# Two ends of a fused LoRA-and-adapter kernel: the first quarter's loads on two queues, and the last batch in half-width accumulators

## Chip, core and metric

The kernel runs on one core of one Trainium2 chip. The metric is device time in microseconds (us). The kernel before takes 432.92 us, the median of three runs (432.73 to 433.76).

## What is computed

Two layers with residuals over x of 8 batches, 256 tokens and 1024 features, all in float32. The first adds a dense product and a gated mixture of eight low-rank experts: the gates are a softmax over the two largest of eight logits, and the logits of one expert per batch get a bias of 5. The second adds a product with one of 16 matrices, picked per batch by an id.

```python
base = jnp.einsum('btd,od->bto', x, W)
logits = jnp.einsum('btd,ed->bte', x, Wr)
logits = logits + 5.0 * jax.nn.one_hot(language_ids, 8)[:, None, :]
topw, topi = jax.lax.top_k(logits, 2)
weights = jax.nn.softmax(topw, axis=-1)
gates = jnp.sum(jax.nn.one_hot(topi, 8) * weights[..., None], axis=-2)
h = jnp.einsum('btd,erd->bter', x, A)
lora_out = jnp.einsum('bter,bte,eor->bto', h, gates, B)                    # 8 experts of rank 16
x = x + base + 2.0 * lora_out
x = x + jnp.einsum('bsi,boi->bso', x, weight[adapter_ids])
```

## The kernel before

The features lie on the 128 partitions. A chunk k is 128 of the 1024 features, so there are eight chunks. The 2048 tokens are cut into four quarters of 512, named (j, c). The input lies in HBM so that one load brings some chunks of one quarter: `load_x(queue, i, j, c, k0, k1)` (line 104) brings chunks k0 to k1 of the half i of the features, so that i = 0 holds chunks 0 to 3 and i = 1 chunks 4 to 7. One chunk of a quarter is 128 rows of 2 KB, 256 KB. `load_aw` (line 112) brings pieces of a table of 136 columns per chunk, which holds the experts' A and the router's Wr side by side; a chunk of it is 68 KB.

The stages, in the order in which TensorE runs them:

- Ten warm-up matmuls on an identity matrix (line 539).
- `project(j, c)`, four times: for each chunk k and each of four groups of 128 tokens one matmul of 128 by 136 columns (line 198). It gives the router's logits and the experts' h of one quarter. After the first quarter's matmuls stands `use_ids()`: VectorE casts the ids to float (line 154), a small matmul spreads them over the partitions (line 156), and VectorE makes the bias from them (lines 158 and 164). The logits get the bias in one addition (line 174), and ScalarE copies h out (line 217).
- The dense product and the LoRA part as seven products of a Strassen-like scheme over 2 by 2 blocks, each of which is itself a scheme of seven steps with accumulators A, B and X (line 374). VectorE makes the sums and differences of blocks (line 174), and results leave PSUM through `evict` (line 360, ScalarE) or an addition (VectorE).
- `adapt(u)` for the eight batches, again seven steps each, of 128 by 512 columns (line 479). `mm` writes an accumulator, `evict` or `add` takes it into the tile z, and `store` (line 491) sends z out. `load_w1` loads the next batches' matrices.

Each engine works through its own queue in the order in which the program was written, and waits on semaphores. Loads are issued from two queues that share the same 16 DMA engines: SP's (`nc.sync`) and ACT's (`nc.scalar`). Eight semaphores are dealt out in turn to the DMAs of these two, so that the ninth load waits until the first has landed: the issue of chunks 4 and 5 of the first quarter waits for the first piece of the table.

The order of the first loads, as written in lines 114 to 126: ACT issues the table in pieces of chunks 0, 1 to 2, and 3 to 7, and after them the two rows of ids (lines 123 and 124). SP issues x chunk 0, chunk 1, chunks 2 to 3, chunks 4 to 5, chunks 6 to 7, and then the second quarter and the rest. Each chunk's matmuls wait for their piece of the table and their piece of x.

The last batch differs in its end: its c22 half is stored early, and the last accumulator, 128 by 512 in one bank of PSUM, is taken out in two halves, one by ScalarE (line 529) and one by VectorE (line 530), each with a store of its own on ACT's and SP's queue.

Of the kernel before, what the change touches and what calls it, by code (L numbers as in the profile page):

```python
# [25 lines left out]
def kernel(  # L26
# [25 lines left out]
    nc = tc.nc  # L52
# [5 lines left out]
    NB = lang.shape[1]  # L58
    NAD = w1.shape[0]
    S = 256  # L60
    KC = D // P
    KH = KC // 2
    TH = NB * S // 2
    TQ = TH // 2
    OG = O // 2
# [3 lines left out]
    SH = S // 2  # L69
# [16 lines left out]
    def bank(name):  # L86
        return psum.tile([P, 2, TQ], F32, name=name, tag="acc")
# [5 lines left out]
    def xk(k, j, c):  # L93

        return xb[f"{k // KH + 1}{j+1}"][:, k % KH, c * TQ : (c + 1) * TQ]
# [5 lines left out]
    ids = const.tile([1, 2, NB], I32, name="ids")  # L101

    def load_x(queue, i, j, c, k0, k1):
        queue.dma_start(  # L104
            xb[f"{i+1}{j+1}"][:, k0:k1, c * TQ : (c + 1) * TQ], xT[i, j, c, :, k0:k1, :]
        )
# [4 lines left out]
    def load_aw(queue, k0, k1):  # L111
        queue.dma_start(aw_sb[:, k0:k1, :], awT[:, k0:k1, :])

    load_aw(nc.scalar, 0, 1)
    load_x(nc.sync, 0, 0, 0, 0, 1)
    load_aw(nc.scalar, 1, 3)
    load_x(nc.sync, 0, 0, 0, 1, 2)
    load_aw(nc.scalar, 3, 8)
    load_x(nc.sync, 0, 0, 0, 2, 4)
    load_x(nc.sync, 1, 0, 0, 0, 2)  # L120
    load_x(nc.sync, 1, 0, 0, 2, 4)
    load_x(nc.sync, 0, 0, 1, 0, 4)
    nc.scalar.dma_start(ids[:, 0, :], lang)
    nc.scalar.dma_start(ids[:, 1, :], adapt)
    load_x(nc.sync, 1, 0, 1, 0, 4)
    load_x(nc.sync, 0, 1, 0, 0, 4)
    load_x(nc.sync, 1, 1, 0, 0, 4)
# [16 lines left out]
    nc.vector.tensor_copy(desc, desc_i)  # L144
    ecol = const.tile([P, E], F32, name="ecol")
    nc.vector.tensor_copy(ecol, ecol_i)
    ids_f = const.tile([1, 2 * NB], F32, name="ids_f")
    bias = const.tile([P, NB, E], F32, name="bias")
    aid_i = const.tile([1, NB], I32, name="aid_i")
# [3 lines left out]
    def use_ids():  # L153
        nc.vector.tensor_copy(ids_f, ids.rearrange("o t b -> o (t b)"))
        wide = bank("ids_wide")[:, 0, :NB]
        nc.tensor.matmul(wide, lhsT=ones, rhs=ids_f[:, :NB], start=True, stop=True)  # L156

        nc.vector.tensor_tensor(
            bias,
            wide.unsqueeze(2).to_broadcast([P, NB, E]),  # L160
            ecol.unsqueeze(1).to_broadcast([P, NB, E]),
            ALU.is_equal,
        )
        nc.vector.tensor_scalar(bias, bias, LANG_BIAS, None, ALU.mult)
# [11 lines left out]
    def add(out_, x, y):  # L176
        tt(out_, x, y, ALU.add)
# [14 lines left out]
    def project(j, c):  # L192

        ps = bank(f"ps_h_{j}_{c}")
        for k in range(KC):
            for r in range(CQ):
                v, u = divmod(r, 2)
                nc.tensor.matmul(  # L198
                    ps[:, v, u * EA : (u + 1) * EA],
                    lhsT=xk(k, j, c)[:, ts(r, P)],  # L200
                    rhs=aw_sb[:, k, :],
                    start=(k == 0 and u == 0),
                    stop=(k == KC - 1),
                    skip_group_check=True,
                )
        if (j, c) == (0, 0):
            use_ids()
        ps = ps[:, :, : 2 * EA].rearrange("p v (u e) -> p v u e", u=2)
        split = lambda t: t[:, c * CQ : (c + 1) * CQ, :].rearrange("p (v u) e -> p v u e", v=2)
        nb = CQ * P // S  # L210
        b0 = (2 * j + c) * nb
        add(
            split(lg[j]),
            ps[:, :, :, ER:],
            bias[:, b0 : b0 + nb, :].unsqueeze(2).to_broadcast([P, nb, CQ // nb, E]),
        )
        nc.scalar.copy(split(hT[j]), ps[:, :, :, :ER])
# [72 lines left out]
    def pump(place, last=7):  # L290

        share = sum(t[0] for t in todo) / (last - place + 1)
        i = 0
        while i < len(todo) and (share > 0.3 or place == last):
            if todo[i][1] > place:
                i += 1
                continue
            us, _, fn = todo.pop(i)
            fn()
            share -= us  # L300
# [4 lines left out]
    def pieces(fn, out_, x, y, n):  # L305

        w = KH // n
        cut = lambda t, c: t[:, c * w : (c + 1) * w, :]
        return [
            (1.22, 0, lambda c=c: fn(cut(out_, c), cut(x, c), cut(y, c))) for c in range(n)  # L310
        ]
# [45 lines left out]
    def evict(dest, acc, base=None):  # L357

        if base is None:
            nc.scalar.copy(dest, acc)  # L360
        else:
            add(dest, acc, base)
# [57 lines left out]
    sums, adapter = {}, {}  # L420
    order = [b for b in range(NB // 2, NB)] + [b for b in range(NB // 2)]

    def load_w1(u, *which):
        if u >= NB:
            return
        if u not in adapter:
            b = order[u]
            adapter[u] = nc.sync.value_load(aid_i[0:1, b : b + 1], min_val=0, max_val=NAD - 1)
        for ij in which:
            i, g = int(ij[0]) - 1, int(ij[1]) - 1  # L430
            nc.sync.dma_start(
                rawset[u % 2][ij], w1[bass.ds(adapter[u], 1), g, i].rearrange("a p k n -> p (a k) n")
            )
# [11 lines left out]
    def yhalf(b):  # L445

        j, r = divmod(b, NB // 2)
        c, s = divmod(r, 2)

        def half(i, k):  # L450
            v = yq(f"{k+1}{j+1}").rearrange("p (r c) m n -> p r c m n", c=2)[:, :, c]
            return v[:, :, :, s * S + i * SH : s * S + (i + 1) * SH]

        return half
# [13 lines left out]
    def adapt(u):  # L468
        b = order[u]
        half = yhalf(b)  # L470
        s1, s2, s3, s4 = sums[u]
        w = rawset[u % 2]
        accs = {}

        def mm(name, lhs, rhs, first=False):
            if first:
                accs[name] = bank(f"{name}1_{u}")[:, 0, :]
            for k in range(KH):
                nc.tensor.matmul(  # L479
                    accs[name],  # L480
                    lhsT=lhs[:, k // 2, k % 2, :],
                    rhs=rhs[:, k, :],
                    start=(first and k == 0),
                    stop=(k == KH - 1),
                    skip_group_check=True,
                )
            return accs[name]

        def store(i, o0=0, o1=O, queue=nc.sync):
            r = b * S + i * SH  # L490
            queue.dma_start(out[r : r + SH, o0:o1], z[i][:, o0:o1])

        z = [
            pool.tile([P, O], F32, name=f"z_{u}_{i}", tag=tag)
            for i, (pool, tag) in enumerate(((sub1, "t1"), (sub1, "t3")) if u % 2 else ((sub2, "t2"), (sub2, "t2")))
        ]
        c11, c12, c21, c22 = (z[i][:, ts(j, OG)] for i in range(2) for j in range(2))
        evict(c11, mm("A", half(0, 0), w["11"], True))
        for t in pieces(minus, w["11"], w["t"], w["11"], 2):
            t[2]()  # L500
        pump(1)
        evict(c22, mm("B", s1, w["12"], True))
        load_w1(u + 2, "12")
        pump(2)
        evict(c12, mm("A", s2, w["t"]))
        for t in pieces(minus, w["t"], w["21"], w["t"], 2):
            t[2]()
        pump(3)
        add(c11, mm("X", half(0, 1), w["21"], True), c11)
        load_w1(u + 2, "21")  # L510
        pump(4)
        add(c22, mm("A", s3, w["11"]), c22)
        if u + 1 == NB:
            store(1, OG, O)
        load_w1(u + 2, "11")
        pump(5)
        add(c12, mm("B", s4, w["22"]), c12)
        store(0)
        load_w1(u + 2, "22")
        pump(6)  # L520
        if u + 1 < NB:
            evict(c21, mm("A", half(1, 1), w["t"]))
            store(1)
            pump(7)
            return

        acc = mm("A", half(1, 1), w["t"])
        m = OG // 2
        nc.scalar.copy(c21[:, :m], acc[:, :m])  # L529
        nc.vector.tensor_copy(c21[:, m:], acc[:, m:])  # L530
        store(1, 0, m, nc.scalar)
        store(1, m, OG)


    ctx.enter_context(tc.manual_schedule())
# [2 lines left out]
    for i in range(WARM):  # L538
        nc.tensor.matmul(idle[:, 0, :P], lhsT=ident, rhs=ident, start=True, stop=True)
    project(0, 0)  # L540
    project(0, 1)
    use_adapter_ids()
    for t in gating(0):
        t[2]()
    project(1, 0)
    add_identity(wb["11"])
    for t in make_subs("1", "11", "11"):
# [46 lines left out]
    for u in range(NB):  # L594
        if u + 1 < NB:
            todo += prep_y(u + 1)
            todo += prep_w1(u + 1, 4)
        adapt(u)
# [48 lines left out]
```

## Time and profile before

| | |
|---|---|
| median of three runs | 432.92 us |
| the profiled execution | 433.07 us |
| its span from first to last instruction | 431.3 us |
| TensorE busy in the span | 424.4 us (98%) |
| VectorE busy | 270.5 us (63%) |
| ScalarE busy | 32.5 us (8%) |
| bytes moved | 55.81 MB, 129 GB/s in the mean |
| queue of SP | 12048 packets, 54.92 MB |
| queue of ACT | 580 packets, 0.69 MB |

The page gives for each group of instructions the line, the engine, the operation, its tiles, the count, the busy time, the mean duration of one and the idle time of the engine before it with what ended that. PE is TensorE's matmuls, PEld its weight loads, DVE is VectorE, ACT is ScalarE, POOL is GpSimd, SP is SyncE; a q behind the name is the sequencer that issues DMAs. One matmul in float32 makes two records. Times in the timeline count from the start of the span.

What the engines did in the stages of the span (for each engine the busy us and the number of records):

```profile
core 0: us, PE busy (x) PEld busy (x) DVE busy (x) ACT busy (x) POOL busy (x), PEclk, DMA share, GB/s
0.00:15.40 15.40, 12.16 (x86) 11.61 (x86) 0.47 (x4) 0.00 (x0) 0.88 (x8) 1.00 0.86 292
15.40:38.00 22.60, 22.60 (x196) 22.59 (x196) 12.18 (x36) 3.25 (x5) 0.00 (x0) 1.00 1.03 400
38.00:235.00 197.00, 197.00 (x472) 88.10 (x471) 141.76 (x156) 10.72 (x12) 0.00 (x0) 1.00 0.12 44
235.00:403.40 168.40, 168.40 (x393) 74.48 (x392) 108.70 (x122) 15.83 (x27) 0.00 (x0) 1.00 0.53 190
403.40:431.30 27.90, 24.24 (x57) 10.45 (x55) 7.40 (x8) 2.72 (x5) 0.00 (x0) 1.00 0.15 57
```

The rows are the first quarter's projection with what lies ahead of it, the other three quarters, the seven products of the first layer, seven batches of the second layer, and the last batch with its stores. In the three middle rows TensorE is busy for the whole of the stage. In the second row the DMA engines are, too: their share is 1.03 at 400 GB/s.

### The profile page before, as it was taken

What the parts mean: (1) busy time and instruction counts of PE and PEld (TensorE: products, weight loads), DVE (VectorE), ACT (ScalarE), POOL (GpSimd) and SP (SyncE); (2) the same over time, 40 slices, a digit from 0 to 9 for tenths busy, and PEclk for the clock granted to TensorE, in tenths of its full rate; (3) what the DMA queues carried; (4) which work ended last, traced back from release to release, by engine and by line L of the source; (5) the groups of instructions that cost most, each with busy time, mean ns of one, the idle gap of its engine ahead of it and who ended that gap; (6) DMA issues with size and microseconds to landing.
All of it is one profiled execution on the core that took longest, in us unless ns stands there. A gap on an engine that the chain in (4) does not pass through costs nothing.

```text
span 431.3 us, 3166 instructions
## 1 busy us (share of the span) xinstructions
PE 424.4 (98%) x1198; PEld 207.2 (48%) x1198; DVE 270.5 (63%) x325; ACT 32.5 (8%) x49; POOL 0.9 (0%) x8
## 2 busy tenths in 40 slices
PE   6999999999999999999999999999999999999996
PEld 6997444444444444444444444444444444444442
DVE  0068695743538887999765775575756576665521
ACT  0112210002000000000000101010110101010110
POOL 0000000000000000000000000000000000000000
PEclk9999999999999999999999999999999999999999
DMA  7995000000002040150202266555738476550202
GB/s 250 390 406 226 0 2 0 0 0 0 2 0 97 14 180 2 52 206 35 97 2 97 97 238 217 216 207 201 286 125 304 157 259 226 198 195 0 97 0 98
DMA packets 12643, 55.81 MB, mean 129 GB/s; under 512 B 1108, under 2 KB 1620, under 8 KB 8020
## 3 DMA queue, kind: packets, MB, share of 16 engines
q1 hardware_dynamic: 12048, 54.92, 35.3%
q10 hardware_dynamic: 580, 0.69, 0.5%
q8 instruction: 9, 0.15, 0.1%
q14 instruction: 6, 0.05, 0.0%
HBM read 47.22 MB, written 8.39 MB: 129 GB/s over the span
## 4 chain that ended last, share of the span: by engine, by line
PE 97%; DMA 2%; SPq 0%; DVE 0%; ACT 0%; issue 0%
PE A L479 25%; PE A L374 24%; PE B L374 14%; PE B L479 13%; PE X L374 7%; PE ps_h L198 7%; PE X L479 6%; DMA x<-xT_dram 2%; PE ps_g L271 0%; SPq L104 0%; DVE z L530 0%; ACT z L529 0%; PE ids_wide L156 0%
## 5 line engine op out<-in xcount | busy, mean ns | idle before, releaser
L479 PE MATMUL B<-x,x 128*128 128x512 f32 x128 | 57.5, 592 | 0.0
L374 PE MATMUL A<-t,s 128*128 128x512 f32 x112 | 50.3, 592 | 0.0
L479 PE MATMUL A<-w,x 128*128 128x512 f32 x96 | 43.2, 592 | 0.0
L479 PE MATMUL A<-w,y 128*128 128x512 f32 x96 | 42.7, 592 | 0.0
L479 PEld LDWEIGHTS B<-x,x 128*128 128x128 f32 x128 | 24.3, 190 | 30.6 <-issue 30.6
L174 DVE TENSOR_TENSOR w<-w,w 128x1024 f32<-128x1024 f32 x24 | 29.1, 1223 | 15.4 <-PE A L479 15.3
L174 DVE TENSOR_TENSOR y<-A,y 128x1024 f32<-128x1024 f32 x22 | 26.9, 1223 | 17.1 <-PE A L374 17.1
L374 PEld LDWEIGHTS A<-t,s 128*128 128x128 f32 x112 | 21.3, 190 | 26.8 <-issue 26.8
L198 PE MATMUL ps_h<-y,x 128*128 128x136 f32 x256 | 30.7, 280 | 1.8 <-DMA y<-awT_dram 1.0
L360 ACT COPY z<-A 128x512 f32<-128x512 f32 x23 | 13.5, 586 | 246.8 <-PE A L479 246.8
L198 PEld LDWEIGHTS ps_h<-y,x 128*128 128x128 f32 x256 | 29.9, 190 | 2.3 <-DMA y<-awT_dram 1.2
L479 PEld LDWEIGHTS A<-w,x 128*128 128x128 f32 x96 | 18.2, 190 | 23.0 <-issue 23.0
L479 PEld LDWEIGHTS A<-w,y 128*128 128x128 f32 x96 | 18.2, 190 | 23.0 <-issue 23.0
L374 PE MATMUL A<-x,w 128*128 128x512 f32 x56 | 25.2, 592 | 0.0
L374 PE MATMUL X<-x,w 128*128 128x512 f32 x56 | 25.2, 592 | 0.0
L374 PE MATMUL B<-x,s 128*128 128x512 f32 x56 | 25.2, 592 | 0.0
L374 PE MATMUL A<-t,w 128*128 128x512 f32 x56 | 25.2, 592 | 0.0
L374 PE MATMUL B<-t,s 128*128 128x512 f32 x56 | 25.2, 592 | 0.0
L174 DVE TENSOR_TENSOR y<-B,y 128x1024 f32<-128x1024 f32 x12 | 14.7, 1224 | 16.3 <-PE B L374 16.3
L174 DVE TENSOR_TENSOR y<-X,y 128x1024 f32<-128x1024 f32 x7 | 8.6, 1226 | 18.0 <-PE X L374 18.0
L174 DVE TENSOR_TENSOR x<-x,x 128x1024 f32<-128x1024 f32 x16 | 18.9, 1218 | 0.0
L174 DVE TENSOR_TENSOR t<-x 128x1024 f32<-128x1024 f32 x14 | 17.1, 1220 | 0.0
(96 smaller groups left out, 378.2 us busy)
## 6 DMA issues: line engine op xcount, KB each, us to landing
x<-w_dram SPq DMA_DIRECT2D x24, 1024.0 KB, 4.8
w<-w_dram SPq DMA_DIRECT2D x8, 1024.0 KB, 4.7
out_dram<-z SPq DMA_DIRECT2D x15, 512.0 KB, 3.3
x<-xT_dram SPq DMA_DIRECT2D x6, 1024.0 KB, 11.2
w<-wT_dram SPq DMA_DIRECT2D x4, 1024.0 KB, 15.6
x<-xT_dram SPq DMA_DIRECT2D x3, 512.0 KB, 6.4
x<-xT_dram SPq DMA_DIRECT2D x2, 256.0 KB, 5.0
b_sb<-bT_dram SPq DMA_DIRECT2D x1, 512.0 KB, 14.8
```

What stands on the lines that cost most here:

```text
L174: nc.vector.tensor_tensor(out_, x, y, op)
L198: nc.tensor.matmul(ps[:, v, u * EA : (u + 1) * EA], lhsT=xk(k, j, c)[:, ts(r, P)], rhs=aw_sb[:, k, :], start=(k == 0 and u == 0), stop=(k ...
L360: nc.scalar.copy(dest, acc)
L374: nc.tensor.matmul(acc[:, m, :], lhsT=l, rhs=r, start=(first and i < 2), stop=(i >= len(steps) - 2), skip_group_check=True,)
L479: nc.tensor.matmul(accs[name], lhsT=lhs[:, k // 2, k % 2, :], rhs=rhs[:, k, :], start=(first and k == 0), stop=(k == KH - 1), skip_group_c ...
```

## The change

Three edits. The first quarter's x loads go out by turns on SP and ACT, chunks 0 to 3 in pieces of one chunk, and the table's last piece moves from ACT to SP. The two rows of ids are issued from GpSimd's queue, behind its own set-up work, and `use_ids()` moves from behind the first quarter's matmuls to before chunk 4. The last batch has a function of its own, `adapt_last`: each step runs as two halves of 256 columns, whose accumulators lie in the two banks of one tile, each half taken out as soon as it is done; the last half leaves through ScalarE alone, and all of its stores are on SP's queue.

```diff
     load_aw(nc.scalar, 0, 1)
     load_x(nc.sync, 0, 0, 0, 0, 1)
     load_aw(nc.scalar, 1, 3)
-    load_x(nc.sync, 0, 0, 0, 1, 2)
-    load_aw(nc.scalar, 3, 8)
-    load_x(nc.sync, 0, 0, 0, 2, 4)
+    load_x(nc.scalar, 0, 0, 0, 1, 2)
+    load_x(nc.sync, 0, 0, 0, 2, 3)
+    load_aw(nc.sync, 3, 8)
+    load_x(nc.scalar, 0, 0, 0, 3, 4)
     load_x(nc.sync, 1, 0, 0, 0, 2)
-    load_x(nc.sync, 1, 0, 0, 2, 4)
+    load_x(nc.scalar, 1, 0, 0, 2, 4)
     load_x(nc.sync, 0, 0, 1, 0, 4)
-    nc.scalar.dma_start(ids[:, 0, :], lang)
-    nc.scalar.dma_start(ids[:, 1, :], adapt)
...
     ecol = const.tile([P, E], F32, name="ecol")
     nc.vector.tensor_copy(ecol, ecol_i)
+    nc.gpsimd.dma_start(ids[:, 0, :], lang)
+    nc.gpsimd.dma_start(ids[:, 1, :], adapt)
...
         for k in range(KC):
+            if (j, c, k) == (0, 0, KH):
+                use_ids()
             for r in range(CQ):
...
-        if (j, c) == (0, 0):
-            use_ids()
...
+        if u + 1 == NB:
+            adapt_last(b, half, sums[u], w, z)
+            return
...
-        if u + 1 == NB:
-            store(1, OG, O)
...
-        if u + 1 < NB:
-            evict(c21, mm("A", half(1, 1), w["t"]))
-            store(1)
-            pump(7)
-            return
-
-        acc = mm("A", half(1, 1), w["t"])
+        evict(c21, mm("A", half(1, 1), w["t"]))
+        store(1)
+        pump(7)
+
+    def adapt_last(b, half, sy, w, z):
+        s1, s2, s3, s4 = sy
         m = OG // 2
-        nc.scalar.copy(c21[:, :m], acc[:, :m])
-        nc.vector.tensor_copy(c21[:, m:], acc[:, m:])
-        store(1, 0, m, nc.scalar)
-        store(1, m, OG)
+        accs = {}
+
+        def mm(name, lhs, rhs, first=False):
+            if first:
+                accs[name] = bank(f"{name}1_last")
+            for v in range(2):
+                for k in range(KH):
+                    nc.tensor.matmul(
+                        accs[name][:, v, :m],
+                        lhsT=lhs[:, k // 2, k % 2, :],
+                        rhs=rhs[:, k, v * m : (v + 1) * m],
+                        start=(first and k == 0),
+                        stop=(k == KH - 1),
+                        skip_group_check=True,
+                    )
+                yield v
...
+        def step(i, j, plus, name, lhs, rhs, first=False):
+            for v in mm(name, lhs, rhs, first):
+                c = place(i, j, v)
+                evict(c, accs[name][:, v, :m], c if plus else None)
+
+        step(0, 0, False, "A", half(0, 0), w["11"], True)
+        for t in pieces(minus, w["11"], w["t"], w["11"], 2):
+            t[2]()
+        step(1, 1, False, "B", s1, w["12"], True)
+        step(0, 1, False, "A", s2, w["t"])
+        for t in pieces(minus, w["t"], w["21"], w["t"], 2):
+            t[2]()
+        step(0, 0, True, "X", half(0, 1), w["21"], True)
+        store(0, 0, OG)
+        step(1, 1, True, "A", s3, w["11"])
+        store(1, OG, O)
+        step(0, 1, True, "B", s4, w["22"])
+        store(0, OG, O)
+        for v in mm("A", half(1, 1), w["t"]):
+            evict(place(1, 0, v), accs["A"][:, v, :m])
+            store(1, v * m, (v + 1) * m)
```

More of the change, by code (lines that the diff above doesn't have):

```diff
@@ L487, in mm, with store @@
             return accs[name]
-        def store(i, o0=0, o1=O, queue=nc.sync):
+        def store(i):
             r = b * S + i * SH
-            queue.dma_start(out[r : r + SH, o0:o1], z[i][:, o0:o1])
+            nc.sync.dma_start(out[r : r + SH, :], z[i])
         z = [
@@ L520, in adapt, with place, store @@
         pump(6)
-        if u + 1 < NB:
-            evict(c21, mm("A", half(1, 1), w["t"]))
-            store(1)
-            pump(7)
-            return
-        acc = mm("A", half(1, 1), w["t"])
-        m = OG // 2
-        nc.scalar.copy(c21[:, :m], acc[:, :m])
-        nc.vector.tensor_copy(c21[:, m:], acc[:, m:])
-        store(1, 0, m, nc.scalar)
-        store(1, m, OG)
+        evict(c21, mm("A", half(1, 1), w["t"]))
[3 more added lines that the diff above has]
+        s1, s2, s3, s4 = sy
+        m = OG // 2
+        accs = {}
[13 more added lines that the diff above has]
+                yield v
+        def place(i, j, v):
+            o = j * OG + v * m
+            return z[i][:, o : o + m]
+        def store(i, o0, o1):
+            r = b * S + i * SH
+            nc.sync.dma_start(out[r : r + SH, o0:o1], z[i][:, o0:o1])
+        def step(i, j, plus, name, lhs, rhs, first=False):
[18 more added lines that the diff above has]
+            store(1, v * m, (v + 1) * m)
     ctx.enter_context(tc.manual_schedule())
```

## The prediction

> **What bounds the kernel now.** I read the page's busy shares first, then the chain that ended last, then the costliest groups with the waits, then the timeline of the two ends.
>
> ```profile
> PE 424.4 (98%) x1198; PEld 207.2 (48%) x1198; DVE 270.5 (63%) x325; ACT 32.5 (8%) x49; POOL 0.9 (0%) x8
> ...
> PE 97%; DMA 2%; SPq 0%; DVE 0%; ACT 0%; issue 0%
> ...
> L198 PE MATMUL ps_h<-y,x 128*128 128x136 f32 x256 | 30.7, 280 | 1.8 <-DMA y<-awT_dram 1.0
> ```
>
> TensorE holds 97% of the chain, and its only idle time above a rounding is 1.8 us before the projection (L198). So a change can gain in two places: those 1.8 us, and what lies after the last matmul. In between TensorE has no gap, so whatever the start gains or loses arrives undiminished at the end. The start, from the timeline of PE (start, duration, group, idle before it):
>
> ```profile
> 5.17 1.13 PE L198 MATMUL ps_h<-y,x 128*128 128x136 f32 x8
> 7.29 1.19 PE L198 MATMUL ps_h<-y,x 128*128 128x136 f32 x8 [0.98 <-DMA y<-awT_dram]
> 9.34 5.83 PE L198 MATMUL ps_h<-y,x 128*128 128x136 f32 x48 [0.86 <-DMA x<-xT_dram]
> 15.10 0.38 PE L156 MATMUL ids_wide<-ids_f,ones 1*128 1x8 f32 x2
> 15.41 0.85 PE L198 MATMUL ps_h<-y,x 128*128 128x136 f32 x5
> ```
>
> A chunk k is four matmuls, eight records. Chunk 0 starts at 5.17 behind the warm-up, chunk 1 waits to 7.29, chunk 2 to 9.34, and chunks 2 to 7 run without a stop: (15.10 - 9.34) / 6 = 0.96 us each. The second block starts at 15.41. When the loads land, from the issues in two short stretches (KB, us from issue to landing; by the timeline of the queues the four of the first stretch were issued at 1.66, 1.67, 1.20 and 1.18, the last one at 5.09):
>
> ```profile
> q1 hardware_dynamic: 317, 0.59, 57.2%
> q10 hardware_dynamic: 275, 0.22, 22.1%
> ...
> x<-xT_dram SPq DMA_DIRECT2D x1, 512.0 KB, 7.6
> y<-awT_dram ACTq DMA_DIRECT2D x1, 340.0 KB, 7.4
> x<-xT_dram SPq DMA_DIRECT2D x1, 256.0 KB, 5.9
> y<-awT_dram ACTq DMA_DIRECT2D x1, 136.0 KB, 6.1
> ...
> x<-xT_dram SPq DMA_DIRECT2D x1, 512.0 KB, 5.6
> ```
>
> So x chunk 1 lands at 7.10, aw 1-2 at 7.28, aw 3-7 at 9.07, x chunks 2-3 at 9.26, x chunks 4-5 at 10.69; the stretch after shows 512 KB in 6.4 from 5.51, chunks 6-7 at 11.91. The first two lines, of 1.5 to 5.5 us, matter most: SP's queue moved 317 packets, 0.59 MB, ACT's 275, 0.22 MB. The queues take turns by packet, not by byte, with ACT slightly behind. The other end:
>
> ```profile
> 427.67 0.37 ACT L529 COPY z<-A 128x256 f32<-128x256 f32 x1 [13.15 <-PE A L479]
> 428.08 0.38 ACTq L491 DMA_DIRECT2D out_dram<-z  x1
> 428.08 0.42 DVE L530 COPY z<-A 128x256 f32<-128x256 f32 x1 [3.08 <-ACT z L529]
> 428.53 0.33 SPq L491 DMA_DIRECT2D out_dram<-z  x1
> ```
>
> PE ends at 427.65. VectorE's half copy waits for ScalarE's half, since both read one accumulator bank. The last store is issued at 428.53, lands 1.9 us later (both final stores show 1.9), and the span ends at 431.3.
>
> **What the Trainium skill says.** "DMA: Bandwidth & Descriptors", section "Queues, rings and completion order": each DMA engine goes round its queue rows packet by packet; the packet counts above agree. Same page, "Issuing engines are not separate DMA queues": issuing from several engines saves only issue time. SP and ACT both carry loads from 0.74 us on already, so a second queue is nothing new here; only what stands at which place in each is. "PSUM — Partial Sum Buffer", "PSUM bank collisions raise a hardware error": two engines may not touch one bank at once, which is why L530 waits for L529. "TensorE: Matmul & The Clock Gate", "Part 1": the clock is halved after an idle window of about 3.4 us; no gap here is that long and the page's clock row is 9 throughout.
>
> **The change part by part.**
>
> Order of first loads. Each piece of one chunk is 128 rows over 16 DMA engines, 8 packets each. Before, rounds of 8 were: x0 with aw0; x1 with aw1-2; half of x2-3 with aw3-7; the rest. So chunk 1 was ready after round 2. After, SP carries x0, x2, aw3-7, then x4-5 (which waits for aw0's semaphore, at 5.09 as now); ACT carries aw0, aw1-2, x1, x3, x6-7. Round 2 is x2 with aw1-2: the same packet sizes as before, so it ends near 7.3, but with chunk 2 landed and not chunk 1. Chunk 1 comes in round 3, beside aw3-7: the bytes of today's round 3, on the lagging queue. So I put it where aw3-7 landed, at 9.07. PE starts chunk 1 at 9.11, where it now starts chunk 2 at 9.34; it is one chunk short, and 0.23 us ahead: 0.96 - 0.23 = +0.73. The bounds: if the 8 packets that x2-3 has alone after aw3-7 cost not the 0.19 between the landings but their full share (256 KB at the 370 GB/s of 7.2 to 9.3, an estimate, 0.71), it is +0.25; if a slow DMA engine delays round 3 by half a us, +1.2.
>
> Is anything later still late? Chunk 2 (landed) runs at 10.07. Chunk 3 at 11.03 needs x3: round 4, 1824 KB in all, between 1568 KB at 9.26 and 2080 KB at 10.69, so about 9.97. Chunk 4 needs x4-5 after round 5; x6-7's first half goes beside it, so 2336 KB: halfway to 2592 KB at 11.91, 11.30, against a start at 11.99. Chunk 6 needs 2848 KB, about 12.5, against 14.22. The second block's 1 MB is as far back in bytes as now (7.26 + 7.6 = 14.86) and is needed at 16.14. All hidden. SP's later loads wait for semaphores of pieces that land up to 1 us later, while the queue is backed up (DMA share 1.0 from 12 to 28 us): nothing.
>
> Ids over GpSimd's queue. Leaves two tiny issues (0.56 and 0.24 us) off ACT, where nobody waits. POOL is free from 1.44 us and nothing stands behind it. ids_wide moves ahead of chunk 4, so PE would wait for ids there: needed at 11.99, landed now before the cast at 7.91. No row of before shows a load on this queue; the DMA page, "Anatomy of one DMA", gives about 2 us fixed. Taken as 0; the cover is 10 us, beyond it each us costs one. Below nothing it cannot go: the 0.31 of the ids matmul is paid in either place while PE is the late side. DVE's bias and lg work moves ahead of the block's end, off the path.
>
> Last batch in halves. 28 matmuls of 512 columns become 56 of 256; records 56 to 112. Today 3.43 us for 8 records of 1024 column passes at 2.4 GHz is 0.429 = 0.4267 + 0.0024. At 512 passes with the same remainder 0.2158: 112 x 0.2158 - 56 x 0.429 = +0.14. No row shows 256 columns. The nearest, 136 columns, makes a record in 0.96 / 8 = 0.120 with its weight load, so weight loads hide below 0.216. Bounds: 0, and +0.7 with a remainder of 0.007 as at 136 columns. The doubled small copies and adds stand beside matmuls; VectorE's and ScalarE's idle before their last rows is 3.1 and 13.1.
>
> The end. The last half's copy is 0.37 alone on ScalarE, then SP issues: 0.02 + 0.37 + 0.04 after PE's end, where it is 0.88 now (428.53 - 427.65). -0.45, with the store's landing unchanged at 1.9. The first half's store goes 1.7 us earlier and clears. What is late next is this copy and the store's own landing.
>
> Sum: +0.73 + 0.14 - 0.45 = +0.42 on the profiled execution's 433.07 (span 431.3 and 1.8 around it): 433.49. It stands 0.15 above the median of 432.92, so I forecast 433.3.
>
> **Rivals.** (1) Chunk 1 does come early: ACT is served by bytes or ahead of SP, and x1 lands near 7.3. For it: ACT's pieces are smaller. Against it: the packet counts. Even then chunks 1 to 3 end by 10.3 and chunk 4 waits for x4-5 at 11.30, which x6-7 now shares the engines with: 11.34 + 4 x 0.96 = 15.18 against 15.41 (ids hidden), so -0.23; in all 433.07 - 0.23 + 0.14 - 0.45 = 432.5, or 432.4 on the median. Only loads about 1 us quicker altogether make it 431.4. (2) Slower, by the clock: PE is idle from 6.30 to 9.11, 2.8 us. If chunk 1 lands after 9.7, the gap is 3.4 us and the clock is halved for the next 3.4 us. The gap costs 0.6 more, the clock 1.7: 433.3 + 2.3 = 435.6. Against it: a gap of 2.8 cannot hold a whole window. (3) The new queue is late: ids land after 11.99. At 13.5 us it is 1.5: 434.8. (4) The edit of the loads does nothing, x1 being as early as now with nothing else moved: only the end, 432.6.
>
> **Numbers.** Forecast 62% (its own range 432.6 to 434.1: start +0.25 to +1.2, end -0.45 to +0.25); (1) 19%, half of it with somewhat quicker loads and so a third of it under 431.6; (2) 8%; (3) 4%; (4) 7%. 0.3%, about what a measurement of this kernel can tell from no change, is 1.3 us: faster lies below 431.6, slower above 434.2. Faster: a third of (1) and a little of (4), 8%. Slower: (2), (3) and the forecast's tail, 13%. Same: 79%. Range 431.9 to 434.2.
>
> **What would show it.** Right: chunk 1's matmuls start near 9.1 with one gap of about 2.8 us put down to x; chunks 1 to 3 run on; ids_wide costs 0.3 before chunk 4; the second block starts near 16.1; each step of the last batch takes 3.45; PE's end to the last issue is 0.43. Wrong: chunk 1 near 7.3, a gap before chunk 4, projection rows at twice their time after the gap, or PE waiting for ids_f. A forecast below 432 fails with the packet turns; one above 434.2 with the clock.

## The result: slower by 5 us, and where the profile after puts it

The changed kernel takes 438.07 us, the median of five runs (437.87 to 438.35), against 433.01 for the kernel before beside it: a ratio of 1.0115, interval 1.01 to 1.013. (Ratios and intervals come from comparing all runs of two kernels, so they differ a little from the ratio of the two medians.) The forecast was 433.3 in a range of 431.9 to 434.2, that is no change that could be told from none; the kernel is 5 us slower. The spans of the two profiled executions are 431.3 and 436.3 us: the whole difference is inside the span.

The page's busy times and chain for the kernel after:

```profile
PE 426.2 (98%) x1254; PEld 217.3 (50%) x1254; DVE 270.6 (62%) x327; ACT 33.4 (8%) x53; POOL 2.0 (0%) x10
...
PE 97%; DMA 1%; ACT 0%; DVE 0%; issue 0%; ACTq 0%; DVEq 0%
```

TensorE is busy 1.8 us more, in 56 more records, and the span is 5.0 us longer. So some 3 us are new idle time of TensorE. The shares in percent do not show it: they still say 98% and 97%. The start is not where the time was lost (timeline of PE, kernel after):

```profile
5.25 1.15 PE L202 MATMUL ps_h<-y,x 128*128 128x136 f32 x8
8.28 3.02 PE L202 MATMUL ps_h<-y,x 128*128 128x136 f32 x24 [1.88 <-DMA x<-xT_dram]
11.23 0.38 PE L158 MATMUL ids_wide<-ids_f,ones 1*128 1x8 f32 x2
11.54 5.71 PE L202 MATMUL ps_h<-y,x 128*128 128x136 f32 x47
```

The two gaps of before, 0.98 and 0.86, have become one of 1.88, and the rest runs without a stop. Before the last batch the kernel after is 0.16 us ahead: its first matmul there starts at 403.44, where that of before starts at 403.60, in the middle of a row of two steps (chain in order of time, before and then after):

```profile
400.17 6.87 PE A L479 x16
...
424.20 3.45 PE A L479 x8
```

```profile
403.44 1.74 PE A_last L540 x8
...
431.04 2.01 PE A_last L540 x8
```

The loss is in the last batch (timeline, kernel after, the last two steps: TensorE's matmuls and the copies and additions between them):

```profile
424.45 1.89 PE L540 MATMUL B_last<-x,x 128*128 128x256 f32 x8
...
426.38 0.42 DVE L176 TENSOR_TENSOR z<-B_last,z 128x256 f32<-128x256 f32 x1 [1.30 <-PE B_last L540]
...
426.86 1.99 PE L540 MATMUL B_last<-x,x 128*128 128x256 f32 x8 [0.52 <-DVE z L176]
...
428.69 1.89 PE L540 MATMUL A_last<-w,y 128*128 128x256 f32 x8
...
430.62 0.37 ACT L362 COPY z<-A_last 128x256 f32<-128x256 f32 x1 [14.18 <-PE A_last L540]
431.04 1.99 PE L540 MATMUL A_last<-w,y 128*128 128x256 f32 x8 [0.46 <-ACT z L362]
433.07 0.37 ACT L362 COPY z<-A_last 128x256 f32<-128x256 f32 x1 [2.08 <-PE A_last L540]
```

Read a step from its first matmul to the next step's. Eight records of the first half, then a gap that ends with the copy (or the addition) of the first half, then the second half. The edit was meant to let the second half's matmuls run beside the first half's copy; the second half waits for it, in every one of the seven steps. TensorE's last record ends at 433.05 in the kernel after and at 427.65 in that of before. So the seven steps take 433.05 - 403.44 = 29.61 us where those of before took 427.65 - 403.60 = 24.05: +5.56. From there to the end of the span it is 436.3 - 433.05 = 3.25 instead of 3.65: -0.40. With the start's -0.16 that is +5.0, the difference of the spans.

### The profile page after: what moved, and what is told of

It reads as the page before. It is cut to its first block, busy times and chain, and to the rows that moved or that the text cites. A ratio compares the mean times of both kernels' runs of the same rounds, so it can differ in the third digit from the quotient of the medians.

```text
span 436.3 us, 3288 instructions
## 1 busy us (share of the span) xinstructions
PE 426.2 (98%) x1254; PEld 217.3 (50%) x1254; DVE 270.6 (62%) x327; ACT 33.4 (8%) x53; POOL 2.0 (0%) x10
## 4 chain that ended last, share of the span: by engine, by line
PE 97%; DMA 1%; ACT 0%; DVE 0%; issue 0%; ACTq 0%; DVEq 0%
PE A L376 24%; PE A L481 22%; PE B L376 14%; PE B L481 11%; PE X L376 7%; PE ps_h L202 7%; PE X L481 6%; PE A_last L540 3%; PE B_last L540 2%; DMA x<-xT_dram 1%; PE X_last L540 1%; ACT z L362 0%; PE ps_g L273 0%; DVE z L176 0%; ACTq L112 0%
## 5 line engine op out<-in xcount | busy, mean ns | idle before, releaser
L481 PE MATMUL B<-x,x 128*128 128x512 f32 x112 | 50.3, 592 | 0.0
L481 PE MATMUL A<-w,x 128*128 128x512 f32 x88 | 39.6, 592 | 0.0
L481 PE MATMUL A<-w,y 128*128 128x512 f32 x88 | 39.1, 592 | 0.0
L481 PEld LDWEIGHTS B<-x,x 128*128 128x128 f32 x112 | 21.3, 190 | 26.8 <-issue 26.8
L362 ACT COPY z<-A 128x512 f32<-128x512 f32 x21 | 12.3, 587 | 241.1 <-PE A L481 241.1
L481 PEld LDWEIGHTS A<-w,y 128*128 128x128 f32 x88 | 16.7, 190 | 21.0 <-issue 21.0
L481 PEld LDWEIGHTS A<-w,x 128*128 128x128 f32 x88 | 16.7, 190 | 21.0 <-issue 21.0
L376 PEld LDWEIGHTS B<-x,s 128*128 128x128 f32 x56 | 10.6, 190 | 13.4 <-issue 13.4
```

The source lines that it names most:

```text
L376: nc.tensor.matmul(acc[:, m, :], lhsT=l, rhs=r, start=(first and i < 2), stop=(i >= len(steps) - 2), skip_group_check=True,)
L481: nc.tensor.matmul(accs[name], lhsT=lhs[:, k // 2, k % 2, :], rhs=rhs[:, k, :], start=(first and k == 0), stop=(k == KH - 1), skip_group_c ...
```

## The experiments

The theory after the result: the loss is one wait per step, for the copy of the first half, and the program sets it because both halves lie in one tile, although in two banks of PSUM; the new loads change next to nothing. The main rival: narrow matmuls, with twice as many weight loads, are slow in themselves. A second one: the start has a gain or a loss of about 1 us, hidden by the other part.

**The loads alone.** The kernel before with the first two edits.

```diff
-    load_x(nc.sync, 0, 0, 0, 1, 2)
-    load_aw(nc.scalar, 3, 8)
-    load_x(nc.sync, 0, 0, 0, 2, 4)
+    load_x(nc.scalar, 0, 0, 0, 1, 2)
+    load_x(nc.sync, 0, 0, 0, 2, 3)
+    load_aw(nc.sync, 3, 8)
+    load_x(nc.scalar, 0, 0, 0, 3, 4)
...
+    nc.gpsimd.dma_start(ids[:, 0, :], lang)
+    nc.gpsimd.dma_start(ids[:, 1, :], adapt)
...
```

> The kernel before with the new order of loads and the ids on GpSimd's queue, last batch as before. Theory (all of the loss is in the last batch; at the start chunk 1 comes a DMA round later and the later chunks follow without a stop, which about cancels): within 0.5 us of before, 432.6 to 433.5. Rival (the loads cost the +0.73 that was forecast and the last batch the rest): 433.6 to 433.9. Rival (the loads gain 1 us or more, hidden behind a larger loss): 431.5 to 432.0.

Measured: 433.13 us against 432.89, a ratio of 1.0002, interval 0.9993 to 1.0011. Neither +0.73 nor a gain of 1 us is inside it (-0.3 to +0.5).

**The last batch alone.** The kernel before with the third edit.

```diff
+        if u + 1 == NB:
+            adapt_last(b, half, sums[u], w, z)
+            return
...
```

> The kernel before with the last batch in halves alone, loads and ids as before. Theory (a wait of TensorE for the first half's eviction in each of seven steps, about 0.8 us each, 0.45 given back at the end): before plus 5.1, 438.0 to 438.4. Rival (start and last batch share the loss): clearly under 437.5.

Measured: 438.07 us against 432.89, 1.0117, interval 1.0103 to 1.0132. All of the loss is here.

**Halves in tiles of their own.** The kernel after; first halves of A and B in the two banks of one tile, second halves in those of another, X's in two more. Same matmuls, same copies, same order.

```diff
             if first:
-                accs[name] = bank(f"{name}1_last")
+                if name != "B":
+                    tiles[name] = [bank(f"{name}1_last_{v}") for v in range(2)]
+                accs[name] = [tiles[{"B": "A"}.get(name, name)][v][:, int(name == "B"), :m] for v in range(2)]
...
```

> The kernel after, with each half's accumulator in a tile of its own (first halves of A and B in the two banks of one tile, second halves in those of another, X's in two more). Theory (the wait is one that is set per tile, though the halves lie in two banks): no gap between the halves, a step at 3.45 to 3.50 us, 432.3 to 433.0. Rival (256-column matmuls with twice the weight loads are slow in themselves, or the waits follow the banks): steps stay near 4.2 us and the time near 438.

Measured: 432.56 us against 432.89, 0.9991, interval 0.9985 to 0.9998. The seven steps of this kernel's last batch in the chain in order of time (start, us, what) and the end of the timeline:

```profile
403.56 10.36 PE A_last L542 x48
413.92 3.45 PE X_last L542 x16
417.38 10.37 PE A_last L542 x48
```

```profile
424.12 3.62 PE L542 MATMUL A_last<-w,y 128*128 128x256 f32 x16
...
426.05 0.37 ACT L362 COPY z<-A_last 128x256 f32<-128x256 f32 x1 [11.71 <-PE A_last L542]
427.77 0.37 ACT L362 COPY z<-A_last 128x256 f32<-128x256 f32 x1 [1.35 <-PE A_last L542]
```

(The first rows carry A's name for B's steps too, which share its tiles.) All 112 records run as one chain, 48 of them in 10.36 us, 3.45 a step. The first half's copy at 426.05 now lies beside the second half's matmuls, and TensorE does not stop for it. The matmuls and weight loads are those of the kernel after, 1254 records of each in both, so the rival falls: it was the tile. Rid of the wait, the change as a whole is worth some 0.3 us.

**Both halves, then out.** The kernel after, one tile, but each step's two halves are computed before either is taken out.

```diff
-            for v in mm(name, lhs, rhs, first):
+            for v in list(mm(name, lhs, rhs, first)):
                 c = place(i, j, v)
...
-        for v in mm("A", half(1, 1), w["t"]):
+        for v in list(mm("A", half(1, 1), w["t"])):
```

> The kernel after, with both halves of a step computed before either is taken out; same matmuls and same one tile. Theory (the wait comes from taking the first half out between the two): steps at 3.45 to 3.50 us, the end as late as before, 432.9 to 433.5. Rival (narrow matmuls and weight loads cost it): near 438.

Measured: 433.12 us against 432.89, 1.0002, interval 0.9994 to 1.0011. In its chain every step but the last is 3.45, and the seven together take 24.19 us, as they do with tiles of their own (427.75 - 403.56): the narrow matmuls cost 24.19 - 24.05 = 0.14.

**One wait.** As that run, but in the last step the first half is taken out between the two.

```diff
-        for v in list(mm("A", half(1, 1), w["t"])):
+        for v in mm("A", half(1, 1), w["t"]):
```

> The kernel after, where steps 1 to 6 of the last batch are taken out after both halves, and only in the last step the first half is taken out between the two. Theory (each eviction between the halves costs TensorE some 0.75 us, seven of them made the loss; in the last step it gives back 0.4 at the end): 0.3 above the run that takes out all after both halves, 433.2 to 433.7. Rival (the loss needs the chain of seven): same as that run or 0.4 below it, 432.7 to 433.1.

Measured: 433.36 us against 433.09, 1.0008, interval 1.0 to 1.0016. The median is 0.24 above that of the run before it, but the kernel before measured beside it is 0.20 higher too, and the two intervals overlap, so the times do not tell the two runs apart. The chain in order of time does:

```profile
420.69 3.45 PE B_last L540 x16
424.14 1.74 PE A_last L540 x8
425.88 0.02 issue
425.91 0.38 ACT z L362
426.29 0.04 issue
426.33 2.01 PE A_last L540 x8
```

The one step with a wait takes 428.34 - 424.14 = 4.20 instead of 3.47: 0.73. Of this 0.44 is the copy and its two handovers, and 0.27 is in the second half itself, 2.01 instead of 1.74. Seven such waits are 5.1; the seven of the kernel after cost 5.42 (29.61 - 24.19). The three that wait for VectorE's additions cost 0.78 to 0.85 each, the four that wait for copies 0.73 to 0.78. So even in the one step where splitting is of use, with one tile it costs 0.73 and saves 0.4 at the end (431.6 - 428.34 = 3.26 from TensorE's last record to the end of the span, against 431.5 - 427.83 = 3.67).

**Chunk 1 and chunk 2 change places** in the loads, with tiles of their own. Now the question is whether the start has more to give.

```diff
-    load_x(nc.scalar, 0, 0, 0, 1, 2)
-    load_x(nc.sync, 0, 0, 0, 2, 3)
+    load_x(nc.sync, 0, 0, 0, 1, 2)
+    load_x(nc.scalar, 0, 0, 0, 2, 3)
```

> The kernel with halves in tiles of their own, and in its loads x chunk 1 and chunk 2 change places (chunk 1 on SP behind chunk 0, chunk 2 on ACT behind the table's second piece). Theory (queues take turns by packet, so the second place of either queue lands a round before the third; then chunks 4 and 5, which share the engines with 6 and 7, set the pace at about 11.3 us): chunk 1 starts at 6.4 to 7.1, a new gap stands before chunk 4, which starts near 11.4, and the time is at most 0.3 us below that with tiles of their own, 432.2 to 432.6. Rival (the first pieces are all that matters at the start): chunk 4 follows without a gap near 10.4 and the time is 431.4 to 431.7.

Measured: 432.46 us against 433.09, 0.9986, interval 0.9977 to 0.9994. Timeline of PE:

```profile
5.39 2.40 PE L202 MATMUL ps_h<-y,x 128*128 128x136 f32 x16
8.33 2.12 PE L202 MATMUL ps_h<-y,x 128*128 128x136 f32 x16 [0.54 <-DMA x<-xT_dram]
10.38 0.38 PE L158 MATMUL ids_wide<-ids_f,ones 1*128 1x8 f32 x2
11.43 6.75 PE L202 MATMUL ps_h<-y,x 128*128 128x136 f32 x56 [0.67 <-DMA x<-xT_dram]
```

As the theory said: chunk 1 follows chunk 0 at once, and a new gap of 0.67 stands before chunk 4, which starts at 11.43 where the kernel after had it at 11.54. Another of 0.54 stands before chunk 2.

**Chunks 6 and 7 behind 4 and 5 on SP,** on top of that, with tiles of their own, and once more in the kernel before without any change of its last batch.

```diff
-    load_x(nc.scalar, 1, 0, 0, 2, 4)
+    load_x(nc.sync, 1, 0, 0, 2, 4)
```

> As the run before, and chunks 6 and 7 go back to SP behind chunks 4 and 5. Theory (by the bytes ahead of it, chunk 4's piece lands near 10 us): no gap before chunk 4, the second block starts at 14.3 to 14.9 instead of 15.5, 431.4 to 432.0. Rival (start-up of the DMA engines, not the order, sets when a piece lands): as with the loads of the change, 432.4 to 432.7.

> The kernel before, its last batch untouched, with ids on GpSimd's queue and the loads of the run before last (chunks 1, 4, 5, 6, 7 on SP, chunks 2 and 3 on ACT). Theory: the gain of the order alone, 0.6 to 1.1 us under before, 431.8 to 432.4. Rival (order of no effect): 432.8 to 433.2.

Measured: 432.67 us against 433.09, 0.9991, interval 0.9983 to 0.9999; and for the loads alone 433.04 against 433.09, 0.9999, interval 0.999 to 1.0007. The theory missed: no gain. The gap had moved again, to chunks 2 and 3, and chunk 4 starts at 11.50 and 11.77 (timeline of PE of the first of the two):

```profile
8.66 1.19 PE L202 MATMUL ps_h<-y,x 128*128 128x136 f32 x8 [0.66 <-DMA x<-xT_dram]
10.09 1.17 PE L202 MATMUL ps_h<-y,x 128*128 128x136 f32 x8 [0.24 <-DMA x<-xT_dram]
11.19 0.38 PE L158 MATMUL ids_wide<-ids_f,ones 1*128 1x8 f32 x2
11.50 6.75 PE L202 MATMUL ps_h<-y,x 128*128 128x136 f32 x56
```

The load of chunks 4 and 5 no longer waits for a semaphore in this order (SP issues it at 2.14 us, and not at 5.27 as in the run before), so it shares the engines with chunk 3, which lands at 10.0.

**Chunks 4 and 5 on ACT, 6 and 7 on SP,** with chunks 1 and 2 changed over and tiles of their own as above, and then the same with only accumulator A in halves.

```diff
-    load_x(nc.sync, 1, 0, 0, 0, 2)
-    load_x(nc.scalar, 1, 0, 0, 2, 4)
+    load_x(nc.scalar, 1, 0, 0, 0, 2)
+    load_x(nc.sync, 1, 0, 0, 2, 4)
```

> Halves in tiles of their own and chunk 1 and 2 changed over, and now chunks 4 and 5 take ACT's place behind chunk 3 while 6 and 7 go to SP. Theory (a piece lands by the packets ahead of it in both queues; before, 6 and 7 landed at 10.2 from that place and 4 and 5 at 11.4): no gap before chunk 4, second block at 14.4 to 14.8, 431.5 to 432.0, about 0.7 below the run with the two chunks changed over. Rival (all orders end at the same 15.3, since what counts is the sum of bytes before the last chunks): 432.3 to 432.6.

> As the run before, but only accumulator A is in halves (two tiles), B and X in whole width of 512. Theory (a step in halves costs 0.02 more than a whole one): 0.1 below the run before, not to be told from it, 431.4 to 432.0. Rival (the halves of B and X also gave something): above it by more than 0.3.

Measured: 432.26 us against 433.00, 0.9980, interval 0.9972 to 0.9988; and 432.29, 0.9983, interval 0.9975 to 0.9991. These two have the lowest times of all, 0.2% under the kernel before. The timeline of PE of the first:

```profile
5.84 4.91 PE L202 MATMUL ps_h<-y,x 128*128 128x136 f32 x32
10.68 0.38 PE L158 MATMUL ids_wide<-ids_f,ones 1*128 1x8 f32 x2
11.34 6.87 PE L202 MATMUL ps_h<-y,x 128*128 128x136 f32 x57 [0.28 <-DMA x<-xT_dram]
```

Its theory missed in part: chunks 0 to 3 run on, but a gap of 0.28 is left before chunk 4, and the time lies above the 432.0 that it allowed, next to the rival's 432.3. The second time is 0.03 above the first, so halves of B and X are worth nothing that can be measured. Whether these loads or only the tiles make them better than the run with tiles of their own (0.9985 to 0.9998) stays open, as the intervals touch.

**The kernel before once more,** profiled only.

> The kernel before, profiled again. Theory (the 9.07 us at which the table's last piece landed in the first profile was one slow DMA engine; in the run with the last batch alone changed it was 8.5): the chunks from 2 on start at 8.6 to 9.0. Rival (9.3 is what this order gives): 9.2 to 9.4.

Measured: 433.27 us, and the timeline of PE has

```profile
5.84 2.81 PE L198 MATMUL ps_h<-y,x 128*128 128x136 f32 x16
9.51 5.83 PE L198 MATMUL ps_h<-y,x 128*128 128x136 f32 x48 [0.86 <-DMA x<-xT_dram]
```

My theory of one chance slow DMA engine fails: chunk 2 starts at 9.51, later than in the first profile (9.34); in the run with the last batch alone changed, the same loads had it at 8.85. The scatter is real, but 9.3 is no outlier for this order.

## Why the prediction was wrong, step by step

Term by term, forecast against measured: the start +0.73 against -0.16, the last batch +0.14 against +5.56, the end -0.45 against -0.40.

**The last batch in halves: the failed step.** It said that the doubled small copies and adds "stand beside matmuls" and priced the edit at +0.14. The price of the matmuls was exact: 24.19 against 24.05, +0.14. The forecast took a record of 256 columns as half of one of 512 but for a small remainder, 0.2158, and 24.19 / 112 is 0.216. What failed is the overlap, whose price was put at nothing: the cover was named without asking whether the program lets the two run beside each other. The second half's first matmul waits for the copy or addition of the first half, 0.73 to 0.85 us in each of seven steps. It was taken for granted that different banks mean no wait; the Trainium skill ("PSUM — Partial Sum Buffer", "PSUM bank collisions raise a hardware error") says that accesses to different banks run clean, and with tiles of their own the copy at 426.05 does lie beside the matmuls, so the chip has no objection. The wait is the program's, and it goes by the tile: the same matmuls and copies with other tiles take 432.56 us. It cost 5.42 us, on the path that sets the end, where TensorE has no slack at all. The kernel before had a sign of such a wait, VectorE's half copy behind ScalarE's. The prediction put it down to the bank; both halves lay in one bank of one tile there, so that row could not tell the two apart, and no run tried to.

**The end: right.** The forecast was 0.43 from PE's end to the last issue and -0.45. Measured in the kernel after: PE's end at 433.05, the copy at 433.07 for 0.37, the last issue at 433.47, and the span's end 0.40 closer to PE's end than before.

**The start: right in outline, wrong in one term.** One gap instead of two, put down to x; chunks 1 to 3 without a stop; the ids matmul 0.31 before chunk 4; chunk 4's piece near 11.30 (issued at 5.18, landed 6.2 later): all as forecast. The term that was mis-sized is chunk 1's landing, taken from where the table's last piece landed before, 9.07. In the kernel after it is 1.68 + 6.5, 8.1 to 8.2 (issues of the kernel after):

```profile
x<-xT_dram ACTq DMA_DIRECT2D x2, 256.0 KB, 6.5
...
y<-awT_dram ACTq DMA_DIRECT2D x1, 136.0 KB, 5.3
...
x<-xT_dram SPq DMA_DIRECT2D x1, 512.0 KB, 6.2
```

So chunk 1 starts at 8.28, not 9.11. In the other runs with these loads it is 8.22 to 8.48, five profiles in all.

Most of the 0.93 us was there a round earlier. The forecast let round 2 end near 7.3, as before, since the same bytes stand ahead of it. But ACT's second piece, issued at 1.19, landed 5.3 later, at 6.5; in the five profiles it is 6.4 to 6.6, and in the three with the order of before 6.7, 7.3 and 7.4. From there to ACT's third piece it then took 1.65 in the kernel after and 1.79 before. Why round 2 came earlier stays open: up to 7 us both kernels had moved the same 1.40 MB, so it was not more bytes, and with the order of before the landing scatters by 0.7. What ACT's queue (q10) and SP's (q1) moved from 7 to 8 us in the kernel after may explain the small rest:

```profile
q10 hardware_dynamic: 214, 0.40, 102.5%
q1 hardware_dynamic: 8, 0.01, 2.9%
```

SP's three pieces had landed by 7.8 and its next load had hardly begun, so ACT's queue had the engines nearly to itself, where before SP's queue moved 171 packets and ACT's 37. That was not tried by itself.

The sum of the start is then not +0.73 but about nothing, -0.3 to +0.5 in the run of the loads alone. That a place further ahead in a queue lands earlier was right, as the run with chunk 1 and 2 changed over shows. "Hidden" was right for the second block and later loads, though chunks 6 and 7, put at 12.5, landed near 10.5, ahead of 4 and 5. Two of the forecast's bounds do not come out of its own figures: the lower one of the start is +0.21 and not +0.25, and its own range is 432.7 to 434.4 and not 432.6 to 434.1. Neither touches the step that failed.

**Ids over GpSimd's queue: right, with less cover than thought.** They landed about 6 us after issue, not 2; the cast ran at 8.06, and PE needed it at 11.23.

**The rivals.** None held the result. Of the signs under "what would show it", a step of the last batch at 3.45 was the one that named the fault: it was 4.2. Chunk 1 near 9.1 with a gap of 2.8 failed too, at 8.28 with 1.88. The rivals for a slower kernel looked for their mechanism at the start, where all my doubts were; the edit with many instructions and a small net price got a single bound, on the speed of a matmul, and none on a wait.

## What to carry to other kernels

When an edit splits a result so that its copy can run beside the next matmuls, ask first what unit the program's dependencies go by: two banks of one tile were one unit here, and each of seven copies and additions stopped the one engine without slack. Give what shall run side by side tiles of its own, and read in the built order what every added instruction waits for before its cost is set to nothing. A wait costs more than the copy that is waited for: 0.73 us for a copy of 0.38, of which 0.27 is that the eight records behind it took longer than without a wait. Why they do was not looked into.

At a start that waits for loads, moving one piece forward moved the gap to another piece: the four new orders of the same loads had the first matmul of chunk 4 at 11.3 to 11.8 us.

## What the runs showed of the hardware that was not expected

Two loads of 32 bytes each on GpSimd's queue took 6.1 and 5.8 us from issue to landing while the other queues were busy; the Trainium skill ("DMA: Bandwidth & Descriptors", "Anatomy of one DMA") names about 2 us of fixed cost for this path, a third of what these two took.

A load that SP issued at 5.18 us, once its semaphore had come, moved next to nothing before 8.2 us: SP's queue has 8 packets from 7 to 8 us and none from 7.6 to 8.2, although only ACT's queue and a few small packets of GpSimd's were at work beside it. The reason was not looked into.

The warm-up of the same ten matmuls took 3.87 to 4.64 us from profile to profile, and chunk 0 started at 5.15 to 5.84. Where it started at 5.84 it could be slow too: 1.97 us for eight records in the run of the loads alone, against 1.15 in the kernel after. It did not reach the end, since the wait for chunk 1 became shorter by as much: chunk 1 started at 8.22 and at 8.28.
